# Final stage of a four-layer image kernel: gate operands by two chunks, turned sums requested from the scans, output tokens four in a row

## The chip, the cores and the metric

The kernel runs on one core of a Trainium2 chip, in one launch. The metric is the device time of that core in microseconds (us); lower is better. Runs of the kernel before gave 3833.25, 3826.19 and 3831.19 us, with a median of 3831.19. The profile comes from one more execution.

Engines are named as the profile names them: PE is TensorE (PEld its weight loads), DVE VectorE, ACT ScalarE, POOL GpSimd, SP SyncE, which here only issues transfers. SPq is SP's queue of commands.

## The reference

Four layers run one after the other on four images of 64x64 tokens with 128 channels, all in float32: a 7x7 neighbourhood attention with a gate, a group norm with full attention over the 4096 tokens, a gated pair layer with a layer norm, and a selective scan in four directions. Only the end of the last layer is touched by the change. Cut to what matters, it is:

```
xz = x @ Win                                  # 128 -> 2 x 256
xb, z = split(xz);  xb = silu(depthwise_3x3(xb))
xs = [xf, xf reversed, xt, xt reversed]       # row order, column order, and both backwards
y_k = selective_scan(xs[k], delta_k, A, B_k, C_k)     # four directions, 256 channels
y = the four y_k brought back to row order, and added
yz = y * silu(z)
xc = yz - yz.mean(-1);  var = (xc * xc).mean(-1)     # over 256 channels
out = (gamma * xc / sqrt(var + 1e-05) + beta) @ Wout  # 256 -> 128
```

The kernel's final stage computes, for each token, the sum of the scan results, its product with the gate, the projection of the 256 channels to 128, and the division by the root of the variance over the 256 channels. The mean is folded into the projection's matrix.

## The kernel before, in words

Layers 0 to 2 run image by image until about 3200 us. Function `layer_3` then has two parts.

**The scans** (pool "s", 3203 to 3661 us). Channels are on the partitions in two halves f of 128; an image is L = 4096 tokens on the free axis, handled in pieces of SC = 1024. Loop `todo` goes over four directions k, in each over four parts (a half f with a pair of images), in each over four pieces. For one piece, ACT makes the step sizes `de`, POOL multiplies them with the input (`inp`, L1210), DVE runs the scan (L1234) and multiplies with the row `cb_s` (`yo`, L1248), and POOL issues a transfer that adds `yo` to a sum (L1249, `y<-yo`, on the software queue q0). Sums of the two row directions lie in DRAM in `y_d[0][b][f]`; those of the two column directions ("turned" sums) lie in DRAM in `y_d[1][b][0]` for f = 0 and in SBUF in `ys[b]` for f = 1. Buffers `cb_s[0]`, `cb_s[1]`, `ub_s[0]`, `ub_s[1]` hold the rows and the inputs of the scans. In the last direction (k = 3) they come free one after the other: `cb_s[0]` after part 1, `ub_s[0]` after part 2, `cb_s[1]` and `ub_s[1]` at the end.

**The final stage** (pool "o", 3661 to 3824 us). It goes over 32 chunks of CH = 512 tokens, eight to an image; the chunk's number is j. Its steps are:

- `load_turned(b)` (L1292): four transfers of 512 KB, issued by SP, bring the turned sums of image b, half 0, into `yts[b]`, which is `cb_s[0]`, `ub_s[0]`, `cb_s[1]`, `ub_s[1]` for b = 0 to 3. In the program it is called for b = 0 and 1 ahead of the loop, for b = 2 at j = 0 and for b = 3 at j = 4.
- `load(j)` (L1301, L1302): for each half f, SP loads `yl` (row sums from `y_d[0]`) and `zc` (the gate from `zf_d`), 256 KB each, into rings of four buffers. Images 1 and 3 are read backwards.
- `add_turned(j)` (L1319): POOL adds the turned sums to `yl`, once per half, into `yc` (ring of three). Of every fourth chunk (j % 4 = 2) half 0 is added by PE instead: ACT copies the turned sums (`back`, L1316), and PE adds in PSUM (`ysum`, L1328).
- `times_gate(j)`: DVE multiplies `yc` with `zc` in place (L1324), or in two halves after `ysum` (L1329, L1330).
- `project(j, p)`, p = 0 and 1, with two groups q of 128 tokens each: PE transposes `yc` into `py` (L1343) so that tokens are on partitions, then multiplies `yc` with `gm` into `po` (L1347); `yc` is the stationary operand of both. `gm` is `gw` with one more column, which gives the mean over the 256 channels. For q = 0 the variance comes from DVE (`bn_stats` L1351, `bn_aggr` L1352). For q = 1 ACT negates and scales the mean (`nm`, L1354) and sums squares (`sq`, L1356).
- `root(j)`: ACT takes the root of the chunk's four variances (`rd`, L1364).
- `give_out(j, p)`: DVE takes the reciprocal (L1370) and scales `po` into `ot` (L1374, four times a chunk); ACT issues the transfer of the chunk to the output (L1379).

The tile framework keeps the written order of instructions for everything inside `pin(...)`, that is for all of the final stage except POOL's adds and the two instructions that make `gm`. It inserts the waits, and it lets instructions of a stage move ahead of earlier ones where the buffers allow it. In round j of the loop stand, in this order: the loads of chunk j+4, the turned loads if due, project(j, 0), give_out(j-1, 0), add_turned(j+2), times_gate(j+1), project(j, 1), root(j), give_out(j-1, 1). Chunks 0 to 2 are loaded at j = -2.

```
for j in range(-2, last + 1):
    for i in range(3) if j == -2 else (j + 4,):
        if i < last:
            load(i)
    if j in (0, 4):
        load_turned(2 if j == 0 else 3)
```

Of the kernel before, what the change touches and what calls it, by code (L numbers as in the profile page):

```python
# [22 lines left out]
F32 = mybir.dt.float32  # L23
# [6 lines left out]
P = 128  # L30
B, H, W, C = 4, 64, 64, 128
L = H * W
# [1079 lines left out]
def layer_3(ctx, tc, of, dt, na, ident, cl, big, early, x3_d, ub_d, zf_d, y_d, dbl_d, ct_d, gw_d, bw_d):  # L1112
# [8 lines left out]
    eps = wp.tile([P, 1], F32, name="eps")  # L1121
    ct = wp.tile([W, 2, W], F32, name="ct")

    def place(name, tag, bufs=1):
        return big.tile([P, L], F32, name=name, tag=tag, bufs=bufs)

# [9 lines left out]
    def turn_c(b, pt):  # L1136

        nc.tensor.transpose(pt, ct[:, 0, :], ident[0:W, 0:W])
        nc.scalar.copy(ct[:, 1, :], pt)
        nc.sync.dma_start(by_rows(bc_d[b][2])[0], ct[:, 1, :])  # L1140
# [6 lines left out]
    def load_c(k, t):  # L1147

        nc.sync.dma_start(cb_s[t], bc_d[k][1 + t][0].partition_broadcast(P))

    def turned(t):

# [16 lines left out]
    with pool("s", 2) as sp, pool("psC", 2, space=PSUM) as psp:  # L1169
# [5 lines left out]
        for k in range(B):  # L1175
            one, two = k & 1, 1 - (k & 1)
            for part, f in enumerate((one, two, two, one)):
                loads = []
                if part == 0:
                    loads = [(load_ub, two, k), (load_c, k, 1)]  # L1180
                elif part == 2 and k + 1 < B:
                    loads = [(load_c, k + 1, 0)]
                elif part == 3 and k + 1 < B:
                    loads = [(load_ub, two, k + 1)]
                for at_n in range(NSC):
                    n = NSC - 1 - at_n if k & 1 else at_n
                    todo.append((loads, [(f, k, 2 * (part >> 1) + q, n) for q in range(2)]))
                    loads = []
# [64 lines left out]
        for j, ((loads, pair), after) in enumerate(zip(todo, todo[1:] + [None])):  # L1253
            for load, *args in loads:
                load(*args)
            coming = deltas(after[1]) if after else None
            hs = [decay(step, de) for step, (de, _) in zip(pair, parts)]
            if late and todo[j][1][0][0:2] != (1, 2):
                nc.gpsimd.dma_start(*late.pop(0), accum_op=ALU.add)
            for step, (_, inp), h in zip(pair, parts, hs):  # L1260
                back(*step, inp, h)
            if j == 0:
                nc.sync.dma_start(gw, gw_d)
                nc.sync.dma_start(bw, bw_d)
                nc.sync.dma_start(ct[:, 0, :], by_rows(bc_d[B - 1][1])[0])
            if j == 18:
                turn_c(B - 1, psp.tile([P, 2, CH], F32, name="pt3", tag="dt0", bufs=1)[0:W, 0, 0:W])
            parts = coming
        assert not late
# [5 lines left out]
    with pool("o", 2) as op, pool("psD", 2, space=PSUM) as psp:  # L1275
        def pin(ins):
            return tc.keep_in_program_order(ins)

        yts = [cb_s[0], ub_s[0], cb_s[1], ub_s[1]]

        gm = op.tile([P, 2, C + 1], F32, name="gm3", tag="gm3", bufs=1)
        nc.gpsimd.memset(gm[:, :, C:C + 1], 1.0 / DI)
        nc.gpsimd.tensor_copy(gm[:, :, 0:C], gw)
        chunks = [(b, n) for b in range(B) for n in range(NCH)]
        held = {}

        class Chunk:
            pass

        def load_turned(b):  # L1290
            for m in range(NSC):
                pin(nc.sync.dma_start(yts[b][:, bass.ts(m, SC)], y_d[1][b][0][m]))  # L1292

        def load(j):
            b, n = chunks[j]
            c = held[j] = Chunk()
            c.yl = op.tile([P, 2, CH], F32, name="yl", tag="yl", bufs=4)
            c.zc = op.tile([P, 2, CH], F32, name="zc", tag="zc", bufs=4)
            lo = L - CH * (n + 1) if b & 1 else CH * n
            for f in range(2):  # L1300
                pin(nc.sync.dma_start(c.yl[:, f, :], y_d[0][b][f][lo // SC][:, lo % SC:lo % SC + CH]))  # L1301
                pin(nc.sync.dma_start(c.zc[:, f, :], zf_d[b][f][:, bass.ts(n, CH)]))  # L1302

        def add_turned(j):


            b, n = chunks[j]
            c = held[j]
            c.yc = op.tile([P, 2, CH], F32, name="yc", tag="yc", bufs=3)
            c.sum = None  # L1310
            for f, yt in enumerate((yts[b], ys[b])):
                yn = c.yl[:, f, ::-1] if b & 1 else c.yl[:, f, :]
                yr = at(yt, 2 | b & 1, CH * n, CH * n + CH)
                if f == 0 and j % 4 == 2:
                    back_t = op.tile([P, CH], F32, name="back", tag="back", bufs=1)
                    pin(nc.scalar.copy(by_rows(back_t), yr))  # L1316
                    c.sum = yn, back_t
                else:
                    nc.gpsimd.tensor_tensor(by_rows(c.yc[:, f, :]), by_rows(yn), yr, ALU.add)  # L1319
# [12 lines left out]
        def project(j, p):  # L1332

            c = held[j]
            if p == 0:
                c.po = []
                c.var = op.tile([P, 4, 2], F32, name="var3", tag="var3", bufs=3)
            py = psp.tile([P, 2, DI], F32, name="py", tag="y", bufs=3)
            po = psp.tile([P, 2, C + 1], F32, name="po3", tag="o", bufs=4)
            for q in range(2):  # L1340
                ts = bass.ts(2 * p + q, P)
                for f in range(2):
                    pin(nc.tensor.transpose(py[:, q, P * f:P * f + P], c.yc[:, f, ts], ident))  # L1343
            for q in range(2):
                ts = bass.ts(2 * p + q, P)
                for f in range(2):
                    pin(nc.tensor.matmul(po[:, q, :], lhsT=c.yc[:, f, ts], rhs=gm[:, f, :], start=(f == 0), stop=(f == 1)))  # L1347


            st = op.tile([P, 6], F32, name="st3", tag="st3", bufs=3)  # L1350
            pin(nc.vector.bn_stats(st, py[:, 0, :]))  # L1351
            pin(nc.vector.bn_aggr(c.var[:, 2 * p, :], st))  # L1352
            nm = op.tile([P, 1], F32, name="nm3", tag="nm3", bufs=3)
            pin(nc.scalar.activation(nm, po[:, 1, C:C + 1], AF.Copy, scale=-1.0 / 16))  # L1354
            sq = op.tile([P, DI], F32, name="sq3", tag="sq3", bufs=2)
            pin(nc.scalar.activation(  # L1356
                sq, py[:, 1, :], AF.Square, bias=nm, scale=1.0 / 16, accum_out=c.var[:, 2 * p + 1, 1:2]
            ))
            c.po.append(po)

        def root(j):
# [4 lines left out]
        def give_out(j, p):  # L1366
# [9 lines left out]
                ))  # L1376
            if p == 1:
                held.pop(j)
                pin(nc.scalar.dma_start(of[b, CH * n:CH * n + CH, :].rearrange("(k p) c -> p k c", p=P), c.ot))  # L1379

        last = len(chunks)
        for b in (0, 1):
            load_turned(b)
        for j in range(-2, last + 1):
            for i in range(3) if j == -2 else (j + 4,):
                if i < last:
                    load(i)
            if j in (0, 4):
                load_turned(2 if j == 0 else 3)
            if 0 <= j < last:  # L1390
                project(j, 0)
            if 0 < j:
# [90 lines left out]
```

## Time and profile before

| | |
|---|---|
| median of three runs | 3831.19 us (3826.19 to 3833.25) |
| profiled execution, its own time | 3828.72 us |
| its span on the core | 3826.9 us |
| layers 0 to 2 | 0 to 3203 us: PE busy 2995.9 |
| scans | 3203 to 3661 us: DVE busy 439.8, POOL 437.1, ACT 429.3 of 458; DMA share 0.96 |
| final stage | 3661 to 3827 us: DVE busy 121.8, PE 109.2, POOL 98.5, ACT 64.9 of 166; DMA share 0.88 |

Busy times are those of one execution. The DMA share is the mean busy share of the core's 16 DMA engines, and GB/s what they moved. In lines of the timeline the columns are start, duration, engine, line of the kernel, operation, output and inputs by the program's names, shape, count, and in brackets the idle time of the engine just before with what ended it. In lines of waits they are the waiting engine and line, what it waited for, the sum in us, how many times, and the longest.

### The profile page before, as it was taken

What the parts mean: (1) busy time and instruction counts of PE and PEld (TensorE: products, weight loads), DVE (VectorE), ACT (ScalarE), POOL (GpSimd) and SP (SyncE); (2) the same over time, 40 slices, a digit from 0 to 9 for tenths busy, and PEclk for the clock granted to TensorE, in tenths of its full rate; (3) what the DMA queues carried; (4) which work ended last, traced back from release to release, by engine and by line L of the source; (5) the groups of instructions that cost most, each with busy time, mean ns of one, the idle gap of its engine ahead of it and who ended that gap; (6) DMA issues with size and microseconds to landing.
All of it is one profiled execution on the core that took longest, in us unless ns stands there. A gap on an engine that the chain in (4) does not pass through costs nothing.

```text
span 3826.9 us, 69375 instructions
## 1 busy us (share of the span) xinstructions
PE 3401.1 (89%) x26780; PEld 2787.6 (73%) x26780; DVE 2829.9 (74%) x4865; ACT 2681.4 (70%) x4350; POOL 1420.2 (37%) x1562
## 2 busy tenths in 40 slices
PE   6999999999899999998999999989999987666647
PEld 4679989966799889667998897669888863222236
DVE  3657777756677788666787886667877866999968
ACT  3865667778676776686766776866767756999934
POOL 5510012245122122352122223522221326999866
PEclk8999999999999999999999999999999996555579
DMA  5100000131010012310211112100101148999998
GB/s 141 47 3 25 12 18 29 43 99 35 18 42 32 32 62 82 121 43 1 74 66 48 51 52 94 46 1 23 41 31 59 57 166 220 232 220 204 213 276 280
DMA packets 205199, 319.30 MB, mean 83 GB/s; under 512 B 23583, under 2 KB 112188, under 8 KB 200732
## 3 DMA queue, kind: packets, MB, share of 16 engines
q1 hardware_dynamic: 165572, 237.57, 18.2%
q0 software_dynamic: 19776, 68.56, 9.8%
q10 hardware_dynamic: 19520, 8.73, 0.8%
q8 instruction: 211, 3.46, 0.4%
q14 instruction: 120, 0.98, 0.1%
HBM read 150.91 MB, written 155.56 MB: 80 GB/s over the span
## 4 chain that ended last, share of the span: by engine, by line
PE 49%; DVE 24%; ACT 9%; POOL 8%; issue 6%; DMA 2%; SPq 1%; POOLq 0%; ACTq 0%; DVEq 0%
PE po L640 15%; PE sc L607 14%; POOL inp L1210 4%; DVE mx L619 4%; DVE acc L858 3%; DVE st L633 3%; POOL y L1249 3%; PE pt L491 3%; DVE mx L614 3%; PE sc L456 2%; PE po L502 2%; ACT st L634 2%; ACT pr L474 2%; ACT st L610 2%; PE pz L808 1%
## 5 line engine op out<-in xcount | busy, mean ns | idle before, releaser
L640 PE MATMUL po<-v,st 128*128 128x129 f32 x8192 | 1081.3, 275 | 4.1 <-ACT st L634 4.1
L607 PE MATMUL sc<-qT,kT 128*128 128x128 f32 x8192 | 1081.9, 276 | 0.4 <-ACT st L610 0.4
L607 PEld LDWEIGHTS sc<-qT,kT 128*128 128x128 f32 x8192 | 1003.5, 193 | 21.9 <-issue 18.1
L640 PEld LDWEIGHTS po<-v,st 128*128 128x128 f32 x8192 | 998.8, 192 | 5.4 <-issue 5.4
L610 ACT COPY st<-sc 128x512 f32<-128x512 f32 x1024 | 577.8, 583 | 527.0 <-PE sc L607 519.6
L633 DVE TENSOR_TENSOR st<-st,pb 128x2048 f32<-128x2048 f32 x256 | 573.9, 2283 | 47.7 <-PE pb L630 47.1
L614 DVE TENSOR_TENSOR mx<-mx,st 128x1024 f32<-128x1024 f32 x256 | 315.3, 1232 | 239.3 <-ACT st L610 237.4
L634 ACT ACTIVATE st<-st 128x2048 f32<-128x2048 f32 x256 | 483.4, 1908 | 6.4 <-DVE st L633 4.7
L1199 PE MATMUL pdt<-dbl,dt 8*128 8x512 f32 x512 | 309.0, 1082 | 142.4 <-ACT de L1206 142.0
L1210 POOL TENSOR_TENSOR inp<-de,ub 128x1024 f32<-128x1024 f32 x128 | 412.1, 4479 | 36.0 <-ACT de L1206 29.0
L1199 PEld LDWEIGHTS pdt<-dbl,dt 8*128 8x128 f32 x512 | 114.4, 312 | 334.1 <-ACT de L1206 270.7
L704 POOL TENSOR_TENSOR x<-x,row 128x512 f32<-128x512 f32 x32 | 49.9, 1559 | 788.9 <-PE pt L274 788.9
L482 POOL TENSOR_SCALAR pr<-pr,sm 128x308 f32<-128x308 f32 (+3 forms) x512 | 243.5, 494 | 259.8 <-DVE sm L480 187.6
L849 POOL TENSOR_TENSOR gsum<-gsum,tp 128x504 f32<-128x504 f32 (+1 forms) x176 | 254.1, 1446 | 122.7 <-ACT gsum L837 83.9
L474 ACT ACTIVATE pr<-pr,mx 128x308 f32<-128x308 f32 (+3 forms) x512 | 262.5, 517 | 0.0
L619 DVE TENSOR_TENSOR mx<-mx 128x512 f32<-128x512 f32 (+2 forms) x384 | 256.9, 669 | 6.1
L1234 DVE TENSOR_TENSOR_SCAN h<-h,end,inp 128x1024 f32<-128x1024 f32 x96 | 221.1, 2346 | 14.7 <-POOL inp L1210 7.0
L491 PE MATMUL pt<-ident,pr 128*88 128x128 f32 (+5 forms) x1472 | 204.1, 276 | 7.8 <-ACT prT L493 7.8
L1249 POOL DMA_DIRECT2D y<-yo x112 | 206.5, 2823 | 7.3 <-DVE yo L1248 3.8
L460 DVE CUSTOM_DVE_ANT_0 pr<-sc,bias_m 128x266 f32<-128x266 f32 (+1 forms) x384 | 151.7, 451 | 69.6 <-PE sc L456 64.7
L858 DVE SCALAR_TENSOR_TENSOR acc<-xh,cc,acc 128x512 f32<-128x512 f32 (+3 forms) x244 | 196.4, 832 | 3.8 <-ACT acc L822 2.7
L491 PEld LDWEIGHTS pt<-ident,pr 128*88 128x88 f32 (+5 forms) x1472 | 163.6, 138 | 45.4 <-ACT prT L493 31.6
(233 smaller groups left out, 5254.7 us busy)
## 6 DMA issues: line engine op xcount, KB each, us to landing
y<-yo POOLq DMA_DIRECT2D x112, 512.0 KB, 10.4
y<-du SPq DMA_DIRECT2D x160, 256.0 KB
zf_d<-zf SPq DMA_DIRECT2D x64, 256.0 KB
ub_d<-u SPq DMA_DIRECT2D x64, 256.0 KB
ub<-ub_d SPq DMA_DIRECT2D x16, 1024.0 KB
yl<-y SPq DMA_DIRECT2D x64, 256.0 KB
zc<-zf_d SPq DMA_DIRECT2D x64, 256.0 KB
x<-in_x SPq DMA_DIRECT2D x128, 64.0 KB
```

Source lines behind the costliest of these rows:

```text
L474: pin(nc.scalar.activation(k.pr[:, h], k.pr[:, h], AF.Exp, bias=k.mx[:, h:h + 1], accum_out=k.sm[:, h:h + 1]))
L491: pin(nc.tensor.transpose(pt[0:n, h, :], k.pr[:, h, at:at + n], ident))
L607: nc.tensor.matmul(ps[:, r, :], lhsT=kT[:, bass.ts(G * g + r, P)], rhs=qT[:, bass.ts(i, P)], start=True, stop=True)
L610: nc.scalar.copy(k.st[:, G * g:G * g + G, :], ps)
L614: nc.vector.tensor_tensor(k.mx, k.mx, k.st[:, 4 * g - 4:4 * g + 4, :], ALU.max)
L619: nc.vector.tensor_tensor(mx[:, 0:n, :], mx[:, 0:n, :], mx[:, n:2 * n, :], ALU.max)
L633: nc.vector.tensor_tensor(part, part, pb.unsqueeze(1).to_broadcast([P, 16, P]), ALU.add)
L634: nc.scalar.activation(part, part, AF.Exp)
L640: nc.tensor.matmul(k.po, lhsT=k.st[:, j, :], rhs=v[:, j, :], start=(j == 0), stop=(j == NT - 1))
L1199: nc.tensor.matmul(pdt[j][:, g, :], lhsT=dt[o:o + RANK, P * f:P * f + P], rhs=at(dbl[o:o + RANK, :], k & 2, g0, g0 + CH), start=True, stop ...
L1210: nc.gpsimd.tensor_tensor(by_rows(inp), by_rows(de), at(ub_s[f], b ^ (k & 1), SC * n, SC * n + SC), ALU.mult)
L1249: nc.gpsimd.dma_start(here if f == 1 and k == 3 else there, yo, accum_op=ALU.add)
```

## The change

The change does the following, all of it in `layer_3`.

1. `gm` moves to the pool that lives through the whole function, and the two POOL instructions that fill it are written into round 18 of the scans.
2. The turned loads of images 0 and 1 are written into the scans, at parts 2 and 3 of the last direction. Those of images 2 and 3 are written one transfer at a time, at even j from 0 to 14, and no turned load is pinned.
3. `yl` and `zc` are loaded for two chunks at once, 512 KB a transfer with rows of 4 KB, into three fixed buffers each; `yc` has three fixed buffers, allocated between them. With the loop as written, `load(4)` is called both at j = -2 and at j = 0.
4. A chunk's groups of 128 tokens are now every fourth token instead of 128 in a row, so that partition p holds tokens 4p to 4p+3, and an output row of a partition is 2 KB in one piece instead of four pieces of 512 bytes.
5. For p = 1 the variance of both groups comes from ACT; DVE's `bn_stats` and `bn_aggr` are left for p = 0, q = 0.

```
--- before.py
+++ after.py
@@ -1121,6 +1121,8 @@
     eps = wp.tile([P, 1], F32, name="eps")
     ct = wp.tile([W, 2, W], F32, name="ct")
 
+    gm = wp.tile([P, 2, C + 1], F32, name="gm3")
+
     def place(name, tag, bufs=1):
         return big.tile([P, L], F32, name=name, tag=tag, bufs=bufs)
 
@@ -1147,6 +1149,12 @@
     def load_c(k, t):
 
         nc.sync.dma_start(cb_s[t], bc_d[k][1 + t][0].partition_broadcast(P))
+
+
+    yts = [cb_s[0], ub_s[0], cb_s[1], ub_s[1]]
+
+    def load_turned(b, m):
+        return nc.sync.dma_start(yts[b][:, bass.ts(m, SC)], y_d[1][b][0][m])
 
     def turned(t):
 
@@ -1182,6 +1190,8 @@
                     loads = [(load_c, k + 1, 0)]
                 elif part == 3 and k + 1 < B:
                     loads = [(load_ub, two, k + 1)]
+                elif part >= 2:
+                    loads = [(load_turned, part - 2, m) for m in range(NSC)]
                 for at_n in range(NSC):
                     n = NSC - 1 - at_n if k & 1 else at_n
                     todo.append((loads, [(f, k, 2 * (part >> 1) + q, n) for q in range(2)]))
@@ -1264,6 +1274,8 @@
                 nc.sync.dma_start(bw, bw_d)
                 nc.sync.dma_start(ct[:, 0, :], by_rows(bc_d[B - 1][1])[0])
             if j == 18:
+                nc.gpsimd.memset(gm[:, :, C:C + 1], 1.0 / DI)
+                nc.gpsimd.tensor_copy(gm[:, :, 0:C], gw)
                 turn_c(B - 1, psp.tile([P, 2, CH], F32, name="pt3", tag="dt0", bufs=1)[0:W, 0, 0:W])
             parts = coming
         assert not late
@@ -1276,37 +1288,41 @@
         def pin(ins):
             return tc.keep_in_program_order(ins)
 
-        yts = [cb_s[0], ub_s[0], cb_s[1], ub_s[1]]
-
-        gm = op.tile([P, 2, C + 1], F32, name="gm3", tag="gm3", bufs=1)
-        nc.gpsimd.memset(gm[:, :, C:C + 1], 1.0 / DI)
-        nc.gpsimd.tensor_copy(gm[:, :, 0:C], gw)
         chunks = [(b, n) for b in range(B) for n in range(NCH)]
         held = {}
 
         class Chunk:
             pass
 
-        def load_turned(b):
-            for m in range(NSC):
-                pin(nc.sync.dma_start(yts[b][:, bass.ts(m, SC)], y_d[1][b][0][m]))
+        def two_chunks(name):
+            return op.tile([P, 2, SC], F32, name=name, tag=name, bufs=1)
+
+
+        spare = place("yl_01", "ring", 5).rearrange("p (a f t) -> p a f t", a=2, f=2)
+        zcs = [two_chunks("zc0")]
+        yc_s = [op.tile([P, 2, CH], F32, name=f"yc{q}", tag=f"yc{q}", bufs=1) for q in range(3)]
+        zcs += [two_chunks("zc1"), two_chunks("zc2")]
+        yls = [spare[:, 0], spare[:, 1], two_chunks("yl2")]
 
         def load(j):
+
             b, n = chunks[j]
-            c = held[j] = Chunk()
-            c.yl = op.tile([P, 2, CH], F32, name="yl", tag="yl", bufs=4)
-            c.zc = op.tile([P, 2, CH], F32, name="zc", tag="zc", bufs=4)
-            lo = L - CH * (n + 1) if b & 1 else CH * n
+            m = n // 2
+            yl, zc = yls[j // 2 % 3], zcs[j // 2 % 3]
             for f in range(2):
-                pin(nc.sync.dma_start(c.yl[:, f, :], y_d[0][b][f][lo // SC][:, lo % SC:lo % SC + CH]))
-                pin(nc.sync.dma_start(c.zc[:, f, :], zf_d[b][f][:, bass.ts(n, CH)]))
+                pin(nc.sync.dma_start(yl[:, f, :], y_d[0][b][f][NSC - 1 - m if b & 1 else m]))
+                pin(nc.sync.dma_start(zc[:, f, :], zf_d[b][f][:, bass.ts(m, SC)]))
+            for h in range(2):
+                c = held[j + h] = Chunk()
+                c.yl = yl[:, :, bass.ts(1 - h if b & 1 else h, CH)]
+                c.zc = zc[:, :, bass.ts(h, CH)]
 
         def add_turned(j):
 
 
             b, n = chunks[j]
             c = held[j]
-            c.yc = op.tile([P, 2, CH], F32, name="yc", tag="yc", bufs=3)
+            c.yc = yc_s[j % 3]
             c.sum = None
             for f, yt in enumerate((yts[b], ys[b])):
                 yn = c.yl[:, f, ::-1] if b & 1 else c.yl[:, f, :]
@@ -1338,24 +1354,28 @@
             py = psp.tile([P, 2, DI], F32, name="py", tag="y", bufs=3)
             po = psp.tile([P, 2, C + 1], F32, name="po3", tag="o", bufs=4)
             for q in range(2):
-                ts = bass.ts(2 * p + q, P)
+                ts = slice(2 * p + q, None, 4)
                 for f in range(2):
                     pin(nc.tensor.transpose(py[:, q, P * f:P * f + P], c.yc[:, f, ts], ident))
             for q in range(2):
-                ts = bass.ts(2 * p + q, P)
+                ts = slice(2 * p + q, None, 4)
                 for f in range(2):
                     pin(nc.tensor.matmul(po[:, q, :], lhsT=c.yc[:, f, ts], rhs=gm[:, f, :], start=(f == 0), stop=(f == 1)))
 
 
-            st = op.tile([P, 6], F32, name="st3", tag="st3", bufs=3)
-            pin(nc.vector.bn_stats(st, py[:, 0, :]))
-            pin(nc.vector.bn_aggr(c.var[:, 2 * p, :], st))
-            nm = op.tile([P, 1], F32, name="nm3", tag="nm3", bufs=3)
-            pin(nc.scalar.activation(nm, po[:, 1, C:C + 1], AF.Copy, scale=-1.0 / 16))
-            sq = op.tile([P, DI], F32, name="sq3", tag="sq3", bufs=2)
-            pin(nc.scalar.activation(
-                sq, py[:, 1, :], AF.Square, bias=nm, scale=1.0 / 16, accum_out=c.var[:, 2 * p + 1, 1:2]
-            ))
+            lo = 1 - p
+            if lo:
+                st = op.tile([P, 6], F32, name="st3", tag="st3", bufs=3)
+                pin(nc.vector.bn_stats(st, py[:, 0, :]))
+                pin(nc.vector.bn_aggr(c.var[:, 2 * p, :], st))
+            nm = op.tile([P, 2], F32, name="nm3", tag="nm3", bufs=3)
+            pin(nc.scalar.activation(nm[:, lo:2], po[:, lo:2, C], AF.Copy, scale=-1.0 / 16))
+            for q in range(lo, 2):
+                sq = op.tile([P, DI], F32, name="sq3", tag="sq3", bufs=2)
+                pin(nc.scalar.activation(
+                    sq, py[:, q, :], AF.Square, bias=nm[:, q:q + 1], scale=1.0 / 16,
+                    accum_out=c.var[:, 2 * p + q, 1:2]
+                ))
             c.po.append(po)
 
         def root(j):
@@ -1376,17 +1396,15 @@
                 ))
             if p == 1:
                 held.pop(j)
-                pin(nc.scalar.dma_start(of[b, CH * n:CH * n + CH, :].rearrange("(k p) c -> p k c", p=P), c.ot))
+                pin(nc.scalar.dma_start(of[b, CH * n:CH * n + CH, :].rearrange("(p k) c -> p k c", k=4), c.ot))
 
         last = len(chunks)
-        for b in (0, 1):
-            load_turned(b)
         for j in range(-2, last + 1):
-            for i in range(3) if j == -2 else (j + 4,):
-                if i < last:
+            for i in (0, 2, 4) if j == -2 else (j + 4,):
+                if i < last and not i & 1:
                     load(i)
-            if j in (0, 4):
-                load_turned(2 if j == 0 else 3)
+            if 0 <= j < 16 and not j & 1:
+                load_turned(2 + j // 8, j // 2 % 4)
             if 0 <= j < last:
                 project(j, 0)
             if 0 < j:
```

## The prediction

> **What bounds the kernel now.** I read the windows over the end of the run first (busy us per engine, granted clock, DMA share, GB/s).
>
> ```profile
> 3656.00:3660.00 4.00, 0.00 (x0) 0.00 (x0) 3.79 (x3) 0.00 (x0) 2.52 (x3) 0.50 1.03 216
> 3676.00:3680.00 4.00, 0.40 (x2) 0.43 (x3) 2.53 (x1) 0.00 (x0) 4.00 (x3) 0.50 1.05 385
> 3690.00:3700.00 10.00, 7.46 (x66) 7.13 (x66) 9.72 (x28) 5.01 (x21) 6.27 (x4) 1.00 0.62 198
> 3752.00:3805.00 53.00, 41.90 (x324) 36.79 (x323) 48.31 (x134) 25.66 (x94) 41.53 (x24) 1.00 1.00 330
> ```
>
> The DMA engines are full from the end of the scans to 3680: first with the scans' last adding writes (216 GB/s), then with loads (385 GB/s, the most I find). From 3752 on DVE is busiest, 48.3 of 53 us. Next, when the gate multiply of a chunk starts (the timeline of DVE); chunks 0, 4, 9, 16 and 20:
>
> ```profile
> 3676.93 2.53 DVE L1324 TENSOR_TENSOR yc<-yc,zc 128x1024 f32<-128x1024 f32 x1 [15.52 <-DMA zc<-zf_d]
> 3695.61 1.74 DVE L1324 TENSOR_TENSOR yc<-yc,zc 128x1024 f32<-128x1024 f32 x1
> 3723.30 1.22 DVE L1324 TENSOR_TENSOR yc<-yc,zc 128x1024 f32<-128x1024 f32 x1 [7.27 <-POOL yc L1319]
> 3755.70 1.75 DVE L1324 TENSOR_TENSOR yc<-yc,zc 128x1024 f32<-128x1024 f32 x1
> 3772.03 1.75 DVE L1324 TENSOR_TENSOR yc<-yc,zc 128x1024 f32<-128x1024 f32 x1
> ```
>
> Four undisturbed chunks take 3772.03-3755.70 = 16.33 us. Chunks 4 to 20 took 76.42 where 4x16.33 = 65.32, so 11.1 us went to late loads; the waits of 3661 to 3752 and, of SP's own queue, of 3690 to 3752 name them (us, times, longest):
>
> ```profile
> POOL yc L1319 <- DMA yl<-y: 11.6, 6, 8.5
> ...
> SPq L1302 <- DMA out<-ot: 14.8, 4, 7.1
> ```
>
> In the second, SP's queue of loads stands still until an output has landed, while the DMA share falls to 0.62. So three parts: start (3661 to 3695.6), stalls (11.1), steady run.
>
> [...] Over 3656 to 3672 the adding queue took most of the time, though against turned loads of 4 KB rows at 3616 to 3618 it got almost nothing:
>
> ```profile
> q0 software_dynamic: 681, 2.46, 83.9%
> q1 hardware_dynamic: 638, 1.18, 20.8%
> ...
> q1 hardware_dynamic: 200, 0.72, 92.5%
> q0 software_dynamic: 10, 0.02, 6.5%
> ```
>
> (3656 to 3672 first; packets, MB, share.) [...] here 2 KB rows already reach 385 GB/s. [...] the gate takes 1.22 us alone and 1.75 to 1.96 beside POOL's adds.
>
> **The change, part by part.**
> - **Early loads of images 0 and 1.** They are written into the scans, but SP already issues them there:
>
> ```profile
> 3613.09 2.16 SPq L1292 DMA_DIRECT2D cb<-y  x4
> 3627.13 1.96 SPq L1292 DMA_DIRECT2D ub<-y  x4
> ```
>
>  They wait for the last readers of those buffers, and still will: 0 us.
> - **The matrix gm** (0.43+0.72 us on POOL) leaves an idle POOL at 3662 and enters the scans, where POOL is nearly full: +0 to 1.15, I take +0.7. Its two waiters on POOL are the next inp and adding write.
> - **Turned loads of images 2 and 3** lose their pin. In the built order of SP's queue seven of the eight now stand ahead of chunk 0's last gate load, six ahead of its first yl. They can start when the last inp ends (3656.8), where the first yl started before. Ahead of gate(0): 7 turned + 2 yl + 2 zc of 0.524 MB = 5.77 MB. Before, plain loads had moved 3.97 MB by 3680 (windows, queue q1). The rest at 385 GB/s takes 1.80/0.385 = 4.7 us, so gate(0) starts at 3684.7, not 3676.9: **+7.8**. If the 4 KB packets crowd the adding writes out, as at 3616, it stays near 3677; at worst I put it at 3690.
> - **Buffer reuse.** Before, chunk 0's first add waited 10.89 us for an adding write, as yc lay over the scans' yo. Now yc is laid elsewhere, and the third yl buffer (chunks 4 and 5) waits for those. That wait of 3673.9 goes; the loads are late in its place.
> - **A load twice.** The loop issues load(4) at the start and again at j=0. SP issues 34+34 loads of 512 KB (yl and zc) where 32+32 would do, and chunk 4 waits for the second copy. Through it stand 23 loads, 12.06 MB: 8.09 MB after 3680, 21.0 us, plus 0.7 for outputs = 3701.7. Counting from gate(0), chunk 4 comes at 3684.7+18.7 (the 18.68 from gate(0) to gate(4) before) = 3703.4. So the copy is hidden by 1.7 us: 0 us, up to +6 if the loads run at the 330 of the steady part.
> - **Two chunks a load.** 512 KB in place of 2x256 KB. [...] Demand is 2.62 MB (2.1 in, 0.52 out) in 8.16 us = 321 GB/s against 385. I expect the 11.1 us of stalls to go: pairs 6, 8 and 10 land near 3711, 3718 and 3725, each just before its need. **-11.1** (bounds 0 and -11.1).
> - **Four tokens in a row.** Output rows are 2 KB instead of 512 bytes: less DMA time, which the steady part hides. TensorE's stationary operand is now read with a stride of 16 bytes. No row shows that. A moving operand with a stride of 256 bytes costs nothing (L1199, eight in 4.78 us at 3211 plain, and at 3440 strided). [...] I take 0; below nothing is excluded, as no fewer bytes are read. Above: see R3.
> - **Statistics of p=1 to ACT.** DVE loses 32x(0.42+0.18) = 19.2 us busy. ACT gains 32 squares of 0.47, pitch 0.56; it is busy 25.66 of 53 us. But DVE still waits for PE and ACT. In a steady chunk now:
>
> ```profile
> 3780.65 0.69 DVE L1329 TENSOR_TENSOR yc<-ysum,zc 128x512 f32<-128x512 f32 x1 [1.11 <-PE ysum L1328]
> ...
> 3781.98 0.17 ACT L1354 ACTIVATE nm<-po 128x1 f32<-128x1 f32 x1 [2.28 <-PE po L1347]
> 3782.38 0.47 ACT L1356 ACTIVATE sq<-py,nm 128x256 f32<-128x256 f32 x1 [0.22 <-DVE st L1351]
> 3782.97 0.30 ACT L1364 ACTIVATE rd<-var,eps 128x4 f32<-128x4 f32 x1
> ```
>
>  With p=1 gone, bn of p=0 follows the gate directly and waits for PE's four transposes, so an ordinary step falls from gate+2.23 to gate+2.05 (two of four: -0.36). After the ysum chunk the reciprocal waits for the root, behind two squares: 2.59 for 2.23, +0.36. The step set by PE stays. Sum **0 per four chunks**, +-0.4, so +-3 over the run. In queue behind that reciprocal are the four ot of DVE; PE waits for their banks only two chunks later. The last root comes 0.56 later: **+0.6**.
>
> **Sum.** From gate(4) to the span's end were 3826.9-3695.6 = 131.3 us; less 11.1 is 120.2. gate(4) at 3703.4 gives 3823.6; +0.6+0.7 = 3824.9, 2.0 below the span before. The profiled execution took 3828.72, 1.8 over its span: 3826.7. The median of the runs, 3831.19, lies 2.5 above it, so about 3829. Some 0.2% (7.7 us) is what a measurement here can tell from no change.
>
> **Rivals.**
> - **R1, loads crowd out the adding writes** (for: the 92.5% at 3616; against: the 20.8% at 3656): gate(0) at 3677, gate(4) at 3695.7, so 7.7 better: about 3821. Chance 0.24.
> - **R2, DVE's relief shortens the period** (for: DVE busy 48.3 of 53; against: PE's sixteen weight loads and matmuls take 3.06 a chunk, with 1.8 for a ysum 14.0 per four, and the step that PE sets stays). From 16.33 to at best 14.2 over seven fours is -15: about 3814. Chance 0.10.
> - **R3, slower: the strided weight load.** If each of PE's transposes and matmuls takes x times its 3.06/16 us, PE per four chunks is 12.24x+1.8; it decides above 16.33, x = 1.19. At 1.5 it is 20.2, +3.8 per four, +31 over eight: about 3858. Between, at 1.3, 17.7, +11. Chance 0.12.
> - **It does not do what it says.** For the early loads this is my main case; then only transfers, order and statistics act.
>
> The main case has 0.54: the bounds of gate(0) (-7.7 to +5), of the stalls (+11) and of the period (+-3) put 0.08 of it faster by over 0.2%, 0.38 within, 0.08 slower. With R1 and R2 less 0.04 that stay within: faster 0.38 (0.08+0.30), within 0.42, slower 0.20 (0.08+0.12). The range, 3815 to 3842, reaches from near R2's best to the main case with the stalls unrelieved (+11) and the period 2 worse; it leaves out most of R3 and the tip of R2.
>
> **What would show it.** Right: gate(0) near 3685, gate(4) near 3703, no wait of SP for an output after 3700, period 16.3, DVE in 53 steady us down by about 8 to 40, LDWEIGHTS unchanged (141 ns for transposes, 192 for the projection). Wrong: turned loads of images 2 and 3 issued after chunk 0's (start), stalls of yc on yl past chunk 8, a period far from 16.3, or LDWEIGHTS above 230 ns.

## The result, and the profile after

The changed kernel takes 3860.88 us (median of four runs, 3858.22 to 3862.89), the kernel before, timed beside it, 3831.84. The ratio is 1.0078, with a 95% interval of 1.0061 to 1.0096: slower by 29 us. The forecast was 3829, range 3815 to 3842.

One window of the changed kernel (busy us of PE, PEld, DVE, ACT, POOL, granted clock, DMA share, GB/s) already holds the answer:

```profile
3752.00:3805.00 53.00, 53.00 (x262) 50.15 (x262) 32.45 (x86) 25.12 (x94) 27.89 (x19) 1.00 0.79 270
```

In the steady stretch TensorE is busy for all of the 53 us, at full clock, and does less in them: 262 matmul records where there were 324. DVE, the busiest before, has fallen from 48.3 to 32.45 us, and the DMA engines are no longer full. The waits of the changed kernel from 3661 us on say who waits for whom (us, times, longest):

```profile
ACT nm L1372 <- PE po L1363: 115.1, 63, 35.8
POOL yc L1335 <- PE po L1363: 59.1, 22, 3.4
...
DVE st L1369 <- PE py L1359: 32.6, 32, 2.4
```

ACT, POOL and DVE all wait for PE. What PE does is seen in the groups by shape, from 3745 to 3835 us (count, busy us, mean ns of one):

```profile
L1363 PE MATMUL po<-gm,yc 128*128 128x129 f32 x288 | 72.7, 395 | 0.0
L1363 PEld LDWEIGHTS po<-gm,yc 128*128 128x128 f32 x288 | 70.0, 327 | 0.0
...
L1359 PEld LDWEIGHTS py<-ident,yc 128*128 128x128 f32 x144 | 24.0, 226 | 1.9 <-PE ysum L1344 1.0 <-issue 0.9
```

The same weight loads had means of 192 and 141 ns before. These overlap (eight with a mean of 192 ns lie in 0.97 us below), so the distance between starts is the better measure. The timeline of the weight loads, first of the kernel before, then of the changed one (start, us, count at the end):

```profile
3786.24 0.42 PEld L1343 LDWEIGHTS py<-ident,yc 128*128 128x128 f32 x4 [1.66 <-issue]
3786.63 0.97 PEld L1347 LDWEIGHTS po<-gm,yc 128*128 128x128 f32 x8
3787.52 0.47 PEld L1343 LDWEIGHTS py<-ident,yc 128*128 128x128 f32 x4
3787.96 0.97 PEld L1347 LDWEIGHTS po<-gm,yc 128*128 128x128 f32 x8
```

```profile
3784.11 0.67 PEld L1359 LDWEIGHTS py<-ident,yc 128*128 128x128 f32 x4
3784.69 1.94 PEld L1363 LDWEIGHTS po<-gm,yc 128*128 128x128 f32 x8
3786.43 0.67 PEld L1359 LDWEIGHTS py<-ident,yc 128*128 128x128 f32 x4
```

Before, the eight passes of `po` took 3787.52-3786.63 = 0.89 us, 111 ns each, and the four of `py` 0.44 us, 110 ns each. Now they take 1.74 us, 217 ns each, and 0.58 us, 145 ns each. One `project` went from 1.33 to 2.32 us. Eight of them and one `ysum` of 1.72 us make 20.3 us, and that is the period of four chunks: the `ysum` gates of chunks 14 and 18 start at 3757.30 and 3777.58 (timeline of DVE), 20.28 us apart, each behind a wait for PE:

```profile
3683.32 2.52 DVE L1340 TENSOR_TENSOR yc<-yc,zc 128x1024 f32<-128x1024 f32 x1 [24.17 <-POOL yc L1335]
3705.09 2.53 DVE L1340 TENSOR_TENSOR yc<-yc,zc 128x1024 f32<-128x1024 f32 x1 [0.24 <-POOL yc L1335]
3757.30 0.69 DVE L1345 TENSOR_TENSOR yc<-ysum,zc 128x512 f32<-128x512 f32 x1 [1.63 <-PE ysum L1344]
3777.58 0.69 DVE L1345 TENSOR_TENSOR yc<-ysum,zc 128x512 f32<-128x512 f32 x1 [1.63 <-PE ysum L1344]
```

The first two lines are gate(0) and gate(4). With them the two profiled executions divide so:

| stretch, us | before | after | difference | predicted |
|---|---|---|---|---|
| to the end of the last `yo` of the scans | 3661.4 | 3659.2 | -2.3 | +0.7 |
| from there to gate(0) | 15.5 | 24.2 | +8.7 | +7.8 |
| gate(0) to gate(4) | 18.7 | 21.8 | +3.1 | 0 |
| gate(4) to the end of the span | 131.3 | 151.3 | +20.0 | -10.5 |
| span | 3826.9 | 3856.4 | +29.5 | -2.0 |

The -2.3 lies ahead of the scans: their first one starts at 3198.26 instead of 3200.58, and both kernels do the same until then. From there to the last `yo` the two take the same time within 0.1 us (460.9 and 460.8).

### The profile page after: what moved, and what is told of

Read it like the earlier page. It is cut to its first block, busy times and chain, and to the rows that moved or that the text cites. A ratio compares the mean times of both kernels' runs of the same rounds, so it can differ in the third digit from the quotient of the medians.

```text
span 3856.4 us, 69277 instructions
## 1 busy us (share of the span) xinstructions
PE 3451.8 (90%) x26780; PEld 2846.4 (74%) x26780; DVE 2811.3 (73%) x4801; ACT 2696.8 (70%) x4414; POOL 1409.4 (37%) x1562
## 4 chain that ended last, share of the span: by engine, by line
PE 52%; DVE 23%; ACT 9%; POOL 8%; issue 6%; DMA 2%; SPq 1%; ACTq 0%; POOLq 0%; DVEq 0%
PE po L640 15%; PE sc L607 14%; DVE mx L619 4%; POOL inp L1220 4%; DVE acc L858 3%; DVE st L633 3%; PE po L1363 3%; POOL y L1259 3%; PE pt L491 3%; DVE mx L614 3%; PE sc L456 2%; PE po L502 2%; ACT pr L474 2%; ACT st L634 2%; ACT st L610 1%
## 5 line engine op out<-in xcount | busy, mean ns | idle before, releaser
L1209 PE MATMUL pdt<-dbl,dt 8*128 8x512 f32 x512 | 308.8, 1082 | 142.6 <-ACT de L1216 142.2
```

The costliest lines, as they stand in the source:

```text
L1209: nc.tensor.matmul(pdt[j][:, g, :], lhsT=dt[o:o + RANK, P * f:P * f + P], rhs=at(dbl[o:o + RANK, :], k & 2, g0, g0 + CH), start=True, stop ...
```

## The experiments

Ratios are against the kernel before, timed on the same chip; medians of the changed kernels are of 4 to 19 runs. "Period" is what four undisturbed chunks take. "Stall" is what gate(4) to gate(28) took beyond six such periods of that arrangement; a dash stands where PE or the strided accesses set a pace above 20 us. Period and stall are read from one profiled execution each, which lay up to 5.4 us from the median of its kernel.

| kernel | median us | ratio, 95% interval | period | stall |
|---|---|---|---|---|
| before | 3829 to 3832 | 1 | 16.33 | 11.1 |
| the change | 3860.9 | 1.0078 (1.0061 to 1.0096) | 20.28 | - |
| change, groups of 128 in a row | 3838.0 | 1.0023 (1.0016 to 1.0030) | 15.9 | 11.8 |
| before, every fourth token | 3853.0 | 1.0058 (1.0041 to 1.0075) | 20.28 | - |
| change, two tokens in a row (8 bytes) | 3832.7 | 1.0004 (0.9996 to 1.0013) | 16.3 | 1.7 |
| change, stride of 32 bytes | 3865.1 | 1.0088 (1.0073 to 1.0103) | 20.5 | - |
| two in a row, load(4) once | 3829.5 | 0.9998 (0.9990 to 1.0007) | 16.3 | 3.9 |
| the same, turned loads late | 3819.7 | 0.9974 (0.9964 to 0.9984) | 16.3 | 6.0 |
| the same, statistics of p=1 on DVE | 3815.4 | 0.9962 (0.9949 to 0.9975) | 16.4 | 1.3 |
| groups in a row, load once, turned late | 3828.5 | 0.9993 (0.9984 to 1.0002) | 15.9 | 19.1 |
| the same, statistics of p=1 on DVE | 3826.8 | 0.9993 (0.9984 to 1.0002) | 16.1 | 11.8 |
| before, two tokens in a row | 3829.6 | 1.0000 (0.9991 to 1.0009) | 16.6 | 8.4 |
| change, yc written in order of groups | 3867.7 | 1.0099 (1.0084 to 1.0114) | about 21 | - |

### Is it the stride of the stationary operand?

The part undone, in the changed kernel:

```
-                ts = slice(2 * p + q, None, 4)
+                ts = bass.ts(2 * p + q, P)
...
-  ... of[...].rearrange("(p k) c -> p k c", k=4) ...
+  ... of[...].rearrange("(k p) c -> p k c", p=P) ...
```

> The changed kernel with one part undone: each group of 128 tokens is again 128 in a row (TensorE's stationary operand contiguous, output rows of 512 bytes). Theory S (the 16-byte stride of the stationary operand is what makes TensorE the bound): projection passes back from 217 to about 111 ns, transposes from 145 to 110 ns, one project from 2.32 to 1.34 us, the period of four chunks from 20.28 to about 16.3 us or less, the time 3825 to 3833 us. Rival A (the two more squares on ACT, or waits around them, hold TensorE back): the period stays above 19 us and the time above 3850 us.

Measured: 3838.0 us, 23 below the change; `po` passes 111 ns apart again, period 15.9. And the opposite diff, put alone into the kernel before:

> The kernel before with one part of the change alone: every fourth token in a group (stationary operand at a stride of 16 bytes) and output rows of 2 KB. Theory S: project 2.32 us, period about 20.3 us, and as part of the 11 us of late loads disappears in the slower pace, +20 to +31 us: 3852 to 3862 us. Rival A: no more than the 2 KB output rows can bring, 3825 to 3833 us.

Measured: 3853.0 us, 24 above its neighbour, period 20.28 to the hundredth as in the change, although here DVE has all its old statistics. Both ends agree: rival A falls, and **the token order alone makes TensorE the bound**. The order brings two things with it, the stride and the output rows of 2 KB. The stride is the cause: a kernel further below keeps the rows of 2 KB with a contiguous stationary operand, and there the weight loads are as short as before (eight in 0.97 us). Token order does not explain all: the run with blocks is still 9 us above before. That rest is followed below, at the start.

### Which stride?

Two tokens in a row, a stride of 8 bytes:

```
-                ts = slice(2 * p + q, None, 4)
+                ts = slice(256 * p + q, 256 * p + 256, 2)
...
-  ... of[...].rearrange("(p k) c -> p k c", k=4), c.ot
+  ... of[...].rearrange("(h p k) c -> p h k c", h=2, k=2), c.ot.rearrange("p (h k) c -> p h k c", h=2)
```

> The changed kernel with two tokens in a row per partition in place of four: the stationary operand has a stride of 8 bytes, output rows are 1 KB. Theory S1 [...]: passes at about 111 ns as with blocks, time within 5 us of the run with blocks. Theory S2 (any stride costs the same): passes 217 ns, about 3860 us. Theory S3 (the cost grows with the stride): passes in between, 130 to 170 ns, 3830 to 3850 us.

And every eighth element of both halves side by side, a stride of 32 bytes:

```
-  ... c.yc[:, f, ts] ...
+  ... c.yc.rearrange("p f t -> p (f t)")[:, 2 * p + q + 4 * f::8] ...
```

> The changed kernel with a stride of 32 bytes for the stationary operand: a group takes every eighth element of both channel halves side by side, so the two halves are mixed and what is projected is not the reference's sum; counts and sizes of all instructions are unchanged. Theories S1 and S2: as at 16 bytes, passes 217 ns, about 3860 us. Theory S3 (cost grows with the stride): passes well above 217 ns; at double, 434 ns, 16 passes a chunk and 32 chunks add 111 us, about 3970 us.

The timeline of the weight loads at 8 bytes, then at 32:

```profile
3765.22 0.68 PEld L1359 LDWEIGHTS py<-ident,yc 128*128 128x128 f32 x4
3765.81 1.03 PEld L1363 LDWEIGHTS po<-gm,yc 128*128 128x128 f32 x8
3766.76 0.56 PEld L1359 LDWEIGHTS py<-ident,yc 128*128 128x128 f32 x4
```

```profile
3772.67 0.65 PEld L1358 LDWEIGHTS py<-ident,yc 128*128 128x128 f32 x4
3773.24 1.99 PEld L1361 LDWEIGHTS po<-gm,yc 128*128 128x128 f32 x8
3775.03 0.63 PEld L1358 LDWEIGHTS py<-ident,yc 128*128 128x128 f32 x4
```

At 8 bytes eight `po` passes take 0.95 us, 119 ns each; at 32 bytes 1.79 us, 224 ns each, hardly more than the 217 at 16. For the projection S2 and S3 fall, and S1's figures nearly hold (119 ns for its 111 at 8 bytes, 224 for its 217 at 32): the cost comes as a step between strides of 8 and 16 bytes, 119 to 217 ns, and hardly grows from there to 32. What makes the step, these runs do not show. A stride of 12 bytes, between the two, was not run. Transposes rise less: four of them take 0.38 to 0.44 us contiguous, 0.47 in most cases at 8 bytes (0.59 in the stretch shown), 0.58 at 16 and 0.57 at 32. Why was not tried.

### Do other operands pay it too?

In this one POOL writes `yc` group by group, so that the stationary operand is contiguous and the output rows still have 2 KB; the gate reads `zc`, and `ysum` its moving operand, at 16 bytes:

```
+  yp = c.yc.rearrange("p f (k t) -> p f k t", k=4);  zp = c.zc.rearrange("p f (t k) -> p f k t", k=4)
+  ... tensor_tensor(yp, yp, zp, ALU.mult) ...
+  ... matmul(ps, lhsT=ident, rhs=part.rearrange("p (t k) -> p k t", k=4), ...) ...
```

> The changed kernel with four tokens in a row and output rows of 2 KB, but the stationary operand contiguous: POOL's adds write yc group by group (a group is then 128 columns in a row), the gate multiply reads zc at a stride of 16 bytes, and the two matmuls of ysum take their moving operand at a stride of 16 bytes. Theory S: project back at 1.34 us, stalls gone, period about 16 us, 3824 to 3830 us if strided access costs DVE and POOL nothing. If 16-byte strides cost DVE as much as the stationary load (gate 1.22 to 2.4 us), period 18 to 19 us and 3840 to 3850 us. The moving operand of ysum: 512 columns in the 0.5 us of a pass now if a moving operand is free of it, 0.87 us if it is read like the stationary one.

The groups by shape of this kernel, 3755 to 3800 us:

```profile
L1345 DVE TENSOR_TENSOR yc<-yc,zc 128x1024 f32<-128x1024 f32 x7 | 17.4, 2490 | 0.0
...
L1335 POOL TENSOR_TENSOR yc<-yl,y 128x512 f32<-128x512 f32 x10 | 17.0, 1700 | 3.8 <-PE po L1368 3.8
L1335 POOL TENSOR_TENSOR yc<-yl,cb 128x512 f32<-128x512 f32 x5 | 14.1, 2817 | 8.5 <-PE po L1368 8.5
...
L1349 PE MATMUL ysum<-yl,ident 128*128 128x512 f32 x4 | 4.0, 1084 | 0.0
```

The gate, with one of its two inputs at 16 bytes, takes 2490 ns where it took 1318 in the change; the `ysum` matmuls have a mean of 1084 ns, 593 in the change and before. POOL's adds have means of 1700 and 2817 ns, 1534 and 1532 in the change, but their scattered writes are not what makes them long. The timelines of POOL and DVE show it:

```profile
3719.11 1.54 POOL L1335 TENSOR_TENSOR yc<-yl,cb 128x512 f32<-128x512 f32 x1 [3.77 <-PE po L1368]
...
3759.51 2.02 DVE L1345 TENSOR_TENSOR yc<-yc,zc 128x1024 f32<-128x1024 f32 x1
...
3770.88 2.83 DVE L1345 TENSOR_TENSOR yc<-yc,zc 128x1024 f32<-128x1024 f32 x1
3771.83 3.31 POOL L1335 TENSOR_TENSOR yc<-yl,cb 128x512 f32<-128x512 f32 x1
```

The add at 3719.11 meets no gate and takes 1.54 us, as long as one without scattered writes (1.53 in the change). The one at 3771.83 begins within a gate, which ends at 3773.71, and it ends 1.43 us after that. From 3755 to 3790 every add above 1.6 us begins within a gate; the others begin outside one, or in its last 0.03 us. So here POOL pays for the longer gates, not for its own stride, and a gate that begins with no add under way takes 2.02 us against 1.22 in the change: that is the price of the stride on DVE.

The stationary operand is contiguous here, the output rows still have 2 KB, and the eight weight loads of `po` are back at half the 1.94 us of the change:

```profile
3767.02 0.97 PEld L1368 LDWEIGHTS po<-gm,yc 128*128 128x128 f32 x8
```

At 3867.7 us it is the slowest of all. The cost was only moved from PE's weight loads to DVE's gate and to `ysum`, and the second, worse case of the expectation was still too low (about 21 us a period).

The `ysum` of this kernel contradicts the row on which the prediction leaned, L1199 of the scans, whose moving operand at 256 bytes cost nothing. Why it did not is measured by changing only the moving operand of `ysum`, in four kinds, in the kernel before:

```
+  rows = (P, 8, 8, P)[j // 4 % 4]          # 256, 256, 16, 16 bytes
+  part = part[0:rows].rearrange(form, j=...)
+  ... matmul(ps, lhsT=ident[0:rows, :], rhs=part, ...)
```

> The kernel before, in which only the moving operand of the matmuls of ysum is changed, to measure it at full clock: for chunks 2 and 18 all 128 rows at a stride of 256 bytes, for 6 and 22 eight rows at 256 bytes, for 10 and 26 eight rows at 16 bytes, for 14 and 30 all 128 rows at 16 bytes (so the turned sums of these chunks are added in another order of tokens, or for 8 rows only, and the outputs of these chunks are not the reference's). A pass of 512 columns takes about 0.43 us contiguous. Theory M1 (the scans' strided row cost nothing because the clock was granted at half there): all four kinds about 0.87 us. Theory M2 (because it read eight rows only): 0.87 us with 128 rows, 0.43 with eight. Theory M3 (because 256 bytes is another case than 16): 0.43 at 256 bytes, 0.87 at 16.

The timeline of PE for chunks 18, 22, 26 and 30, first operand (two passes each; the second operand starts 1.71, 1.80, 1.92 and 1.84 us later):

```profile
3769.76 1.89 PE L1331 MATMUL ysum<-yl,ident 128*128 128x512 f32 x2
...
3787.92 1.97 PE L1331 MATMUL ysum<-yl,ident 8*128 8x512 f32 x2
...
3807.89 2.10 PE L1331 MATMUL ysum<-yl,ident 8*128 8x512 f32 x2
...
3827.63 2.02 PE L1331 MATMUL ysum<-yl,ident 128*128 128x512 f32 x2
```

The contiguous passes of chunk 18 in the kernel before, for comparison, both operands:

```profile
3762.40 1.02 PE L1328 MATMUL ysum<-yl,ident 128*128 128x512 f32 x2
3763.26 1.02 PE L1328 MATMUL ysum<-back,ident 128*128 128x512 f32 x2
```

All four kinds take 0.86 to 0.96 us a pass, twice the 0.43 of a contiguous one. The clock is read from the contiguous passes beside them: eight `po` matmuls take 1.93 us in the kernel before at a granted clock of 0.50 (3680 to 3683) and 1.06 at 1.00 (3686 to 3690), and here ahead of each of the four chunks 1.06, so that those of the first operand began at full clock. Eight rows don't help, 256 bytes don't help: M2 and M3 fall. M1 has direct support in the same run, since chunk 10 (eight rows at 16 bytes, as chunk 26) met half the clock, with eight `po` matmuls in 1.93 us ahead of it and behind it:

```profile
3731.08 2.20 PE L1331 MATMUL ysum<-yl,ident 8*128 8x512 f32 x2
3733.11 1.97 PE L1331 MATMUL ysum<-back,ident 8*128 8x512 f32 x2
```

Its two passes take 3733.11-3731.08 = 2.03 us, 1.02 each, where chunk 26 took 0.96 each: half the clock hardly lengthened a strided pass here. A contiguous one it doubled, from the 0.43 us above: passes of L1199 in the scans, at a granted clock of 0.50, start 0.86 us apart at 3212.5 (contiguous) and 0.87 us apart at 3441.0 (strided), two at a time. So the strided row of the scans cost nothing because a contiguous pass was as slow there. (The means, 1096 ns where L1199 is contiguous and 1082 where it is strided, say the same.) A strided pass at full clock with everything else of the scans was not run.

One thing this probe shows by the way: behind the eight-row passes of chunks 6, 22 and 26 PE ran at half its pace, with eight `po` matmuls in 1.93 us at 3709.57, 3792.46 and 3812.62 where they took 1.06 ahead of them, though PE was busy throughout; behind those with 128 rows (chunks 2, 14, 18 and 30) they took 1.06. Why was not shown. The 3847 us of its single execution are therefore not the price of the stride alone.

### The start: one load twice, and the turned loads

```
-            for i in (0, 2, 4) if j == -2 else (j + 4,):
+            for i in (0, 2) if j == -2 else (j + 4,):
```

> The kernel with two tokens in a row, and the load of chunks 4 and 5 issued once instead of twice (2.1 MB less at the start). The prediction's step (the second copy is hidden behind the start of the first chunks): gate(4) stays near 3704, time within 2 us of the 3832.7 of that kernel. Rival: the copy delays chunk 4 by its transfer time, 2.1 MB at 385 GB/s = 5.4 us: about 3827 us.

Measured: 3829.5 us against 3832.7, with intervals that overlap. The time lies between the two forecasts and does not tell them apart, but the gates do: gate(0) to gate(4) took 19.3 us, 19.4 with the second copy. The prediction's step holds: up to gate(4) the copy is hidden. Whether dropping it saves up to 3 us elsewhere is open.

```
-                load_turned(2 + j // 8, j // 2 % 4)
+                pin(load_turned(2 + j // 8, j // 2 % 4))
```

> As the run before in this list, and the turned loads of images 2 and 3 held to their written places, behind the first three pairs of yl and zc loads. The prediction's step (7 turned loads ahead of chunk 0 cost 7.8 us): gate(0) back from 3685 to about 3677, gate(4) to about 3696, and the time about 8 us below the kernel that issues them early: 3822 to 3826 us. Rival (the start is set by the scans' last adding writes, and the early loads only fill what is free): gate(0) stays near 3684 and the time at 3830 to 3833 us.

Measured: 3819.7 us, 9.8 below the run before it, intervals apart. The first gates of this kernel (timeline of DVE):

```profile
3671.87 1.23 DVE L1340 TENSOR_TENSOR yc<-yc,zc 128x1024 f32<-128x1024 f32 x1 [8.95 <-DMA zc<-zf_d]
3674.88 1.19 DVE L1340 TENSOR_TENSOR yc<-yc,zc 128x1024 f32<-128x1024 f32 x1
```

gate(0) comes 8.95 us after the last `yo`, where it took 24.1 with the early turned loads and 15.5 in the kernel before. So the early loads cost the start, and the 24.1 for 15.5 are the rest left open above by the run with groups of 128 in a row. Of the 15.2 us that gate(0) gains here, 9.8 are left in the medians; stalls of 6.0 for 3.9 us account for two of the difference, the rest is open. Without the early loads the new buffers, whose `yc` no longer lies over `yo`, win 6.6 us over the kernel before, which the expectation had not asked for. POOL's first add, before and in this kernel, shows the wait that has gone; it starts 12.5 and 0.9 us after the last `yo`:

```profile
3673.91 1.51 POOL L1319 TENSOR_TENSOR yc<-yl,cb 128x512 f32<-128x512 f32 x1 [10.89 <-DMA y<-yo]
```

```profile
3663.79 3.30 POOL L1335 TENSOR_TENSOR yc<-yl,cb 128x512 f32<-128x512 f32 x2
```

In the changed kernel SP's timeline shows the order, with the first `yl` behind six turned loads of images 2 and 3 (`cb` is image 2 here, `ub` image 3):

```profile
3654.54 1.49 SPq L1157 DMA_DIRECT2D ub<-y  x2
3656.14 0.95 SPq L1157 DMA_DIRECT2D cb<-y  x2
3657.18 1.89 SPq L1157 DMA_DIRECT2D ub<-y  x1
3659.17 1.68 SPq L1157 DMA_DIRECT2D cb<-y  x1
3660.94 1.42 SPq L1313 DMA_DIRECT2D yl<-y  x1
```

### Rows of the output, and the statistics

> The kernel before with one part alone: two tokens in a row per partition, so output rows of 1 KB instead of 512 bytes, loads by single chunks as before. Theory O (the 11 us of late loads come from the slow landing of 512-byte output rows, which SP's queue waits for): gate(4) to gate(20) falls from 76.4 to about 66, the time to 3817 to 3822 us. Theory W (they come from the number of transfers, five per chunk, whatever their rows): 76 stays, about 3829 us.

The edit is that of two tokens in a row, in the kernel before. Measured: 3829.6 us, no difference; gate(4) to gate(20) took 74.7 us, far from the 66 of theory O, and its period had grown to 16.6. Theory O falls for loads by single chunks.

```
-            lo = 1 - p
+            lo = 1
```

> The kernel with two tokens in a row, one load of chunks 4 and 5, and late turned loads, with one part undone: the variance of p=1, q=0 comes from DVE again. The prediction's step (the move of the statistics gives 0 +-0.4 us per four chunks, and 0.6 at the end): within 3 us of 3819.7. Rival (DVE's relief sets the pace): the period grows from 16.3 by the two instructions per chunk, 4x0.6 = 2.4 us per four, and the time by about 17 us, 3837.

Measured: 3815.4 us, period 16.4 for 16.3. It is the fastest kernel of the study, 0.38% (0.25 to 0.51) below the kernel before. The rival falls: DVE's 0.6 us a chunk are not missed. The 4.3 us in favour of DVE lie within overlapping intervals.

> The changed kernel with all three of its costs undone: groups of 128 tokens in a row (contiguous stationary operand, output rows of 512 bytes), one load of chunks 4 and 5, turned loads held late. If contiguous operands decide: period 15.9 for 16.3 us, 2 to 3 us below 3819.7. If the landing of 512-byte output rows decides, which SP's queue waits for: stalls of some 8 us more than with 1 KB rows, 3824 to 3828 us.

Measured: 3828.5 us. The period is the shorter one, 15.9, but the stalls are 19.1 us. Whether the rows or ACT make them is told by the same kernel with the statistics on DVE:

> The kernel with 128 tokens in a row per group, output rows of 512 bytes, one load of chunks 4 and 5 and late turned loads, with the variance of p=1, q=0 again from DVE. It differs in the output's rows alone (and the contiguous stationary operand) from the one that took 3815.4 us with 1 KB rows, and in the statistics alone from the one that took 3828.5. Theory E (512-byte output rows land late, and SP's loads wait for them, whoever computes the statistics): stalls of 10 us or more from gate(4) on, 3824 to 3829 us. Theory F (the later roots and outputs that come of two squares on ACT make the loads late): stalls below 3 us, period 16.3, 3813 to 3818 us.

Measured: 3826.8 us and 11.8 us of stalls, against 3815.4 and 1.3 with rows of 1 KB. Theory F falls. Theory E, that late outputs are the cause, fits both kernels, with one limit: they differ in the stationary operand too, contiguous here and at 8 bytes there, so that PE's pace is a little faster here (16.1 for 16.4). A kernel with a contiguous operand and 1 KB rows was not run. The waits of SP's queue from 3690 to 3800, first with 1 KB, then with 512 bytes:

```profile
SPq L1313 <- DMA out<-ot: 44.7, 15, 6.0
```

```profile
SPq L1313 <- DMA out<-ot: 48.8, 8, 10.2
```

The sums are alike, but the longest wait of a `yl` load for an output is 6.0 us in one and 10.2 in the other. What it costs is seen in the compute engines that wait for a transfer in the same stretch, again first with 1 KB, then with 512 bytes:

```profile
DVE ot L1394 <- DMA out<-ot: 0.2, 1, 0.2
```

```profile
POOL yc L1335 <- DMA yl<-y: 7.2, 2, 4.8
DVE ot L1394 <- DMA out<-ot: 5.1, 6, 1.7
```

With 1 KB these waits make 0.2 us, with 512 bytes 12.3, about what the stalls differ by. Outputs delay the kernel in two ways: SP's loads wait for them, and so does DVE, before it writes into an `ot` that has not left yet. The output queue itself (3700 to 3790 us; packets, MB, share of the 16 engines), before with 512 bytes, the kernel of 3815.4 us with 1 KB, the change with 2 KB:

```profile
q10 hardware_dynamic: 10040, 4.99, 18.6%
```

```profile
q10 hardware_dynamic: 6007, 5.79, 18.4%
```

```profile
q10 hardware_dynamic: 2451, 4.46, 13.1%
```

Per full share of 90 us that is 298, 350 and 378 GB/s. The rows decide this, not the rest of the kernel: over the same stretch the other kernels give 290 to 297 with 512 bytes, 350 to 352 with 1 KB and 372 to 378 with 2 KB.

## Why the prediction was wrong

- **The failed step is "Four tokens in a row": "I take 0".** It cost 24 us alone, and turned DVE's end stretch into PE's. Two things went wrong in it. The comparison with L1199 took a row at half clock (0.50 granted) for evidence at full clock; at full clock a moving operand at 16 or 256 bytes took twice the time as well (0.86 to 0.96 us a pass for 0.43). And of the stationary operand at 16 bytes it said itself "No row shows that": with no row of its own to set against a cost, R3 deserved more than 0.12. A pass of the projection took 217 ns there, 111 contiguous.
- **R3 was the case that came.** Its place (the weight loads of the final stage), its test (those of the projection above 230 ns) and its time (3858 for a measured 3860.9) were right, the last partly by luck: it took 1.5 times 1.53 us a project, where it was 1.74 times 1.33, and it spread the cost evenly over passes, where the projection's doubled and the transposes' rose by a third. Its 31 us on the main case's 3829 would have been 3860; 3858 is 31 on the 3826.7 of a profiled execution. The steady part gave 20.28 for its 20.2.
- **The start was right.** gate(0) was forecast at 3684.7 and came at 3683.3, gate(4) at 3703.4 and came at 3705.1, though with PE already behind part of the last. Counted from the last `yo` gate(0) is 8.7 us later than before, 7.8 was forecast. R1 falls: the first `yl` stood behind the turned loads and nothing made up for it. The second copy was hidden, as said. That the loads would be late in place of the adding writes was said too; what the sum had no figure for is that 6.6 us were free there, had the turned loads been held back.
- **"Two chunks a load: -11.1" was wrong in its cause.** With two-chunk loads and 512-byte rows the stalls stay at 11.8 to 19.1 us; with two-chunk loads and 1 KB rows they fall to 1.3 to 6.0. 1 KB rows with single-chunk loads leave 8.4. Both are needed, and the prediction credited the first alone. Its sign, no wait of SP for an output after 3700, failed in every kernel looked at: even the fastest has 44.7 us of such waits of `yl` loads from 3690 to 3800; they only cost nothing there. The output queue with rows of 512 bytes, at 298 GB/s, was the slowest of the three. In the changed kernel itself the slow PE hid the question.
- **The statistics were right.** 0 +-0.4 us per four chunks was forecast; the pairs show 16.4 and 16.3, 16.1 and 15.9. R2 falls: with PE at its old rate and DVE relieved the period never went below 15.9.
- **The early turned loads of images 0 and 1 and gm** left no mark: the scans took 460.9 us for 460.8; +0.7 had been put down for `gm`.

## What to carry to other kernels

A stride in the free axis of an operand had a price here where it was read: at 16 bytes PE paid it on its stationary operand (217 ns for 111 a pass of the projection) and on its moving one (0.86 to 0.96 us for 0.43 a pass), DVE on one input of two (2.02 us for 1.22). So ask at what distance an instruction reads its floats: 8 bytes were nearly free in the passes of the projection (119 ns), 16 cost about twice the time, and 32 hardly more (224). Before a row of the profile is taken as proof that something is free, look at the granted clock of its stage: at 0.50 the passes of L1199 started 0.86 us apart contiguous and 0.87 strided, which hid what PE paid at full clock. A long instruction can also be the victim of another: here POOL's adds grew from 1.54 us to 3.31 where DVE's longer gate was running. A load that has lost its fixed place in a queue can move ahead of the one that the next stage is waiting for, as six turned loads did here (gate(0) 24.2 us after the last `yo` for 15.5): the order of issue has to be read from the built program.

## What was not expected of the hardware

- A moving operand at 16 or 256 bytes doubled a pass of `ysum` too (0.43 to 0.86 us or more), with 8 rows as with 128; smaller strides were not tried on it. At half the clock the same strided pass took about as long, 1.02 for 0.96 us. DVE's gate with one input of two at 16 bytes took 2.02 us for 1.22. A POOL add with scattered writes took 1.54 us, the same as without, where no gate of DVE was running when it began, and 3.31 where one was.
- Passes of the projection doubled (111 to 217 ns), while transposes of the same data rose by a third (110 to 145). This stays open.
- Output rows of 512 bytes, 1 KB and 2 KB moved at 298, 350 and 378 GB/s of the engines' time; with loads of two chunks rows of 512 bytes took 11 us longer than rows of 1 KB (3826.8 for 3815.4, part of it possibly by PE's pace), with loads of single chunks there was no difference in time (a ratio of 1.0000). Why is open.
